# Layer 0's cross-attention: the query and key weights multiplied once, and tokens projected through the product

## The chip, the core and the metric

The kernel runs on one core of a Trainium2 chip. The metric is the device time of one execution in microseconds; 844.53 us is the median of three runs before the change (841.44 to 846.62). The core has TensorE (PE: matmuls and transposes), VectorE (DVE), ScalarE (ACT), GpSimd (POOL) and SyncE (SP), whose queue here issues all DMA transfers. Each engine works through its own list in order and waits on semaphores for the others.

## The reference

Two layers of cross-attention and feed-forward over x (8 batches of 128 tokens of 512) and a context of the same shape. The change touches only the first attention:

```
x = x + xattn0(layernorm(x), ctx)

def xattn0(text, features, Wq, bq, Wk, bk):
    Q = einsum('btx,dx->btd', text, Wq) + bq
    K = einsum('bpx,dx->bpd', features, Wk) + bk
    scores = einsum('btd,bpd->btp', Q, K) / sqrt(512)
    attn = softmax(scores, axis=-1)
    return einsum('btp,bpd->btd', attn, features)
```

Wq and Wk are 512x512; there is one head and no projection of the values. Then come a low-rank adapted FFN with a gate (layer 0), an attention with 32 query and 8 key/value heads of 128, and a gated FFN with integer weights (layer 1). Layer 1's keys and values are projected from the same context.

## The kernel before

The 1024 tokens are held as two halves of 512 (`HB` = 4 batches of `P` = 128; `KT` = 4 blocks of 128 channels). Float32 operands of the projections are split in two reduced-precision parts, h + l (`split_fast` lines 64 to 66: ScalarE casts h, VectorE subtracts to get l; `split_pool` 60 to 62 and `split_both` 68 to 70 use GpSimd), and a product is three matmuls, h·l, h·h and l·h (`mm3`, lines 77 to 80). A projection of one half is thus 4 output tiles x 4 k x 3 = 48 matmuls of 128x512.

A layer-0 half is a generator, `layer0(hf)` (line 195). Its first part normalises the tokens: statistics on VectorE (line 84, 86), the inverse deviation on GpSimd (88, 89), the normalised tokens on VectorE (95), four transposes on TensorE (101), a cast on ScalarE (107) and a remainder on VectorE (108), for each of four batches. Then it projects the half's context to keys: half 0 by `proj_first` (line 181), which goes k by k over four PSUM banks so that it can follow the loads, half 1 by `proj_T` (line 170). The bias is added where ScalarE empties PSUM (179, 193). The second part projects the tokens to queries (202). The third part multiplies queries and keys in float32 (208), takes the row maximum (212), scales it (214) and exponentiates (218). Later parts multiply by the context (236) and compute the FFN.

The loads stand ahead (lines 313 to 347): half 0's context and Wk, transposed on the host, block by block in turn; the tokens; the two biases as columns of 4; Wq. Half 1's context follows behind the first part of half 0 and is split by ScalarE and GpSimd (337). Then come FFN biases, gate and low-rank weights. The split WT (FFN) takes the place of Wk when that is done with (350).

In the built program each DMA issue on SP also waits for the landing of the transfer eight before it. Outside of the stages that are ordered by hand (from line 909) a scheduler interleaves the engines' lists. It mixes the context's projections for layer 1 (`kv_part`, line 395: matmuls `kv`, 128x256, from the split context `cT` and `wkv`) into layer 0 as filler for TensorE.

Of the kernel before, what the change touches and what calls it, by code (L numbers as in the profile page):

```python
# [21 lines left out]
HB = 4  # L22
TOK = HB * P
# [11 lines left out]
def f32(ap):  # L35
    return ap.bitcast(F32)
# [3 lines left out]
def tile_layers(ctx: ExitStack, tc: tile.TileContext, t, out: bass.AP):  # L40
    nc = tc.nc

    def pool(stack, name, bufs, space=None, side="left"):
        kw = {"side": side}
        if space is not None:
            kw["space"] = space
        return stack.enter_context(tc.tile_pool(name=name, bufs=bufs, reuse_waits="tile", **kw))

    const = pool(ctx, "const", 1)
    stage = pool(ctx, "stage", 3)  # L50
    small = pool(ctx, "small", 3)
    big = pool(ctx, "big", 2)
    dram = ctx.enter_context(tc.tile_pool(name="dram", bufs=1, space=bass.MemoryType.DRAM))
# [10 lines left out]
    def split_fast(h, lo, src):  # L64
        nc.scalar.copy(h, src)
        nc.vector.tensor_tensor(lo, src, f32(h), ALU.subtract)

    def split_both(h, lo, src):
        nc.scalar.copy(h, src)
        nc.gpsimd.tensor_tensor(lo, src, f32(h), ALU.subtract)  # L70
# [8 lines left out]
        nc.tensor.matmul(o, ah, bh, start=False, stop=False)  # L79
        nc.tensor.matmul(o, al, bh, start=False, stop=stop)  # L80

    def layernorm_stats(x):
        st = small.tile([P, 6], F32, name="bnst")
        nc.vector.bn_stats(st, x)
        mv = small.tile([P, 2], F32, name="mv")
        nc.vector.bn_aggr(mv, st)
        rstd = small.tile([P, 1], F32, name="rstd")
        nc.gpsimd.tensor_scalar(rstd, mv[:, 1:2], 1.0, LN_EPS, ALU.mult, ALU.add)
        nc.gpsimd.tensor_tensor(rstd, rstd, nhalf[:, 0:1], ALU.pow)
        return mv, rstd  # L90

    def layernorm_x(x, stats=None):
        mv, rstd = stats or layernorm_stats(x)
        xn = stage.tile([P, D], F32, name="xn", bufs=2)
        nc.vector.tensor_scalar(xn, x, mv[:, 0:1], rstd, ALU.subtract, ALU.mult)
        return xn

    def layernorm_t(xn, nh, nl, cols, ps_tr, extra=None):
        tp = ps_tr.tile([P, KT, P], F32, name="tr")
        for k in range(KT):  # L100
            nc.tensor.transpose(tp[:, k, :], xn[:, k * P : (k + 1) * P], ident)
        if nh is not None:
            layernorm_cut(tp, nh, nl, cols, extra)
        return tp
# [4 lines left out]
        if extra is not None:  # L109
            nc.scalar.copy(extra[:, :, cols], tp)  # L110

    def layernorm_T(hf, ps_tr, extra=None):

        nh = big.tile([P, KT, TOK], F32R, name="xnT_h")
        nl = big.tile([P, KT, TOK], F32R, name="xnT_l")
        for b in range(HB):
            layernorm_t(layernorm_x(xs[hf][:, b, :]), nh, nl, slice(b * P, (b + 1) * P), ps_tr, extra)
        return nh, nl


# [2 lines left out]
    xs = [const.tile([P, HB, D], F32, name=f"xs{hf}") for hf in range(2)]  # L123
# [17 lines left out]
    ps_tr = pool(sln, "ps_tr", 2, PSUM, "right")  # L141
    ps_s = pool(s0, "ps_s", 1, PSUM)
    ps_mm = pool(s0, "ps_mm", 2, PSUM)

    wts = {}

    def tile_w0(nm):
        wts[nm] = tuple(
            w0.tile([P, KT, D], F32R, name=("wq0_" if nm == "WqT" else "wkf0_") + p) for p in "hl"
        )  # L150

    tile_w0("WqT")
    tile_w0("WkT")

    def load_w0(nm, split):
# [4 lines left out]
    bq_sb = w0.tile([P, KT], F32, name="bq_sb")  # L160
    bk_sb = w0.tile([P, KT], F32, name="bk_sb")
# [18 lines left out]

    def proj_first(w, src, bias, dst):

        pss = [ps_mm.tile([P, TOK], F32, name="mm") for _ in range(2)]
        pss += [ps_kv.tile([P, 2, 2 * HD], F32, name="kv").rearrange("p a b -> p (a b)") for _ in range(2)]
        for k in range(KT):
            for j, ps in enumerate(pss):
                cols = slice(j * P, (j + 1) * P)
                mm3(
                    ps, w[0][:, k, cols], w[1][:, k, cols], src[0][:, k, :], src[1][:, k, :],
                    k == 0, k == KT - 1,  # L190
                )
        for j, ps in enumerate(pss):
            nc.scalar.activation(dst[:, j, :], ps, AF.Identity, bias=bias[:, j : j + 1])

    def layer0(hf):
        xt = xs[hf]
        xn = layernorm_T(hf, ps_tr)
        kT = l0.tile([P, KT, TOK], F32, name="k0T", bufs=2)
        (proj_T if hf else proj_first)(wts["WkT"], (cTh[hf], cTl[hf]), bk_sb, kT)
        yield  # L200
        qT = l0.tile([P, KT, TOK], F32, name="qx", bufs=2)
        proj_T(wts["WqT"], xn, bq_sb, qT)
        yield
        sp = ps_s.tile([P, HB, P], F32, name="s")
        for b in range(HB):
            cols = slice(b * P, (b + 1) * P)
# [36 lines left out]
        nh, nl = layernorm_T(hf, ps_tr, xf)  # L243
# [4 lines left out]
        for b in range(HB):  # L248
            cols = slice(b * P, (b + 1) * P)
# [53 lines left out]
        for b in range(HB):  # L303
            cols = slice(b * P, (b + 1) * P)
            ps = ps_mm.tile([P, D], F32, name="mm")
# [4 lines left out]
            nc.vector.tensor_tensor(xt[:, b, :], ps, xt[:, b, :], ALU.add)  # L310


    wk_st, cT_st = (l0.tile([P, KT, TOK], F32, name="qx", bufs=2) for _ in range(2))
    wq_st = l0.tile([P, KT, TOK], F32, name="k0T", bufs=2)
# [6 lines left out]
    nc.sync.dma_start(bk_sb, t["bk"])  # L321
    nc.sync.dma_start(bq_sb, t["bq"])
    for k in range(KT):
        nc.sync.dma_start(wq_st[:, k, :], t["WqT"][k * P : (k + 1) * P, :])
    h, lo = wts["WkT"]
    for k in range(KT):
        split_fast(cTh[0][:, k, :], cTl[0][:, k, :], cT_st[:, k, :])
        split_fast(h[:, k, :], lo[:, k, :], wk_st[:, k, :])
    h, lo = wts["WqT"]
    for k in range(KT):  # L330
        split_fast(h[:, k, :], lo[:, k, :], wq_st[:, k, :])
    A, B = layer0(0), layer0(1)
    next(A)
    c1_st = l0.tile([P, KT, TOK], F32, name="qx", bufs=2)
    for k in range(KT):
        nc.sync.dma_start(c1_st[:, k, :], t["ctxT"][k * P : (k + 1) * P, TOK : 2 * TOK])
        split_both(cTh[1][:, k, :], cTl[1][:, k, :], c1_st[:, k, :])
# [143 lines left out]
    qps, qss, rqs, qbs, pbs, q_d, p_d, qTs, sps, nms, sms, prs, tps, pTs, avs, aTs, pos = ({} for _ in range(17))  # L481
# [278 lines left out]
    for i in range(3 * NI):  # L760
        m, c = MS[i % 3], i // 3
# [38 lines left out]
    def norm_stats(b):  # L800
        xst[b] = layernorm_stats(xs[b // HB][:, b % HB, :])
# [306 lines left out]
    with tc.manual_schedule(engines={ET.PE, ET.DVE, ET.Activation, ET.Pool}):  # L1108

        c = ORDER[-1]  # L1110
# [100 lines left out]
```

## Time and profile before

| | |
|---|---|
| median of three runs | 844.53 us |
| profiled execution, its own time | 844.08 us |
| its span on the core | 842.3 us |
| TensorE busy | 820.1 us |
| VectorE busy | 634.8 us |
| DMA, mean | 196 GB/s |
| first matmul of the span | 5.19 us |
| keys of half 0, matmuls (line 193 empties them) | 5.19 to 18.5 us |
| keys of half 1, with eight transposes | 19.3 to 31.4 us |
| queries of half 0 begin | 32.91 us |
| last score of half 0 | 61.8 us |

The profile is one execution. Busy time is counted per engine, and the durations of single instructions overlap on TensorE, so the distance from one matmul to the next is the better measure there. A wait names the engine whose signal came last.

### The profile page before, as it was taken

What the parts mean: (1) busy time and instruction counts of PE and PEld (TensorE: products, weight loads), DVE (VectorE), ACT (ScalarE), POOL (GpSimd) and SP (SyncE); (2) the same over time, 40 slices, a digit from 0 to 9 for tenths busy, and PEclk for the clock granted to TensorE, in tenths of its full rate; (3) what the DMA queues carried; (4) which work ended last, traced back from release to release, by engine and by line L of the source; (5) the groups of instructions that cost most, each with busy time, mean ns of one, the idle gap of its engine ahead of it and who ended that gap; (6) DMA issues with size and microseconds to landing.
All of it is one profiled execution on the core that took longest, in us unless ns stands there. A gap on an engine that the chain in (4) does not pass through costs nothing.

```text
span 842.3 us, 14135 instructions
## 1 busy us (share of the span) xinstructions
PE 820.1 (97%) x4312; PEld 694.1 (82%) x4312; DVE 634.8 (75%) x1064; ACT 515.8 (61%) x1691; POOL 597.3 (71%) x609
## 2 busy tenths in 40 slices
PE   7999999999989999999999999999999989999996
PEld 6889998898878888888888888888888867778775
DVE  6805897675667777777777777777798897998987
ACT  6524542255666676667677666767676668755663
POOL 3713882235677887787778777888886768797686
PEclk9999999999999999999999999999999999999999
DMA  8613532274789988788888888887877602232202
GB/s 311 138 68 109 181 118 84 69 237 145 252 254 295 289 275 269 260 282 278 257 271 275 257 265 283 286 271 251 291 235 249 204 23 75 75 88 75 63 27 100
DMA packets 153564, 164.96 MB, mean 196 GB/s; under 512 B 15632, under 2 KB 94224, under 8 KB 153488
## 3 DMA queue, kind: packets, MB, share of 16 engines
q1 hardware_dynamic: 153488, 164.06, 61.3%
q8 instruction: 34, 0.56, 0.3%
q14 instruction: 42, 0.34, 0.1%
HBM read 104.78 MB, written 59.24 MB: 195 GB/s over the span
## 4 chain that ended last, share of the span: by engine, by line
PE 74%; DVE 8%; POOL 6%; DMA 5%; issue 4%; ACT 2%; SPq 1%; POOLq 0%; DVEq 0%; ACTq 0%
PE mm L78 8%; PE mm L80 8%; PE mm L79 8%; PE f L982 7%; PE f L983 7%; PE o L644 6%; PE o L647 6%; PE o L645 6%; PE s L575 5%; PE kv L78 2%; PE kv L79 2%; PE kv L80 2%; PE o L623 2%; PE o L624 1%; PE o L625 1%
## 5 line engine op out<-in xcount | busy, mean ns | idle before, releaser
L589 ACT ACTIVATE pr<-s,nm 128x128 f32<-128x128 f32 x256 | 90.5, 365 | 49.6 <-DVE nm L583 45.8
L78 PE MATMUL mm<-wq_l,xnT_h 128*128 128x512 f32 x256 | 105.6, 412 | 0.4 <-DVE q L544 0.2
L644 PE MATMUL o<-wo_l,aT_h 128*128 128x512 f32 x256 | 100.0, 391 | 2.3 <-DVE xs L652 2.3
L616 POOL TENSOR_TENSOR pT_l<-pT,pT_h 128x512 fp32r<-128x512 f32 x64 | 82.9, 1295 | 27.3 <-ACT pT_h L615 24.6
L80 PE MATMUL mm<-wq_h,xnT_l 128*128 128x512 f32 x256 | 101.3, 396 | 0.0
L79 PE MATMUL mm<-wq_h,xnT_h 128*128 128x512 f32 x256 | 100.7, 393 | 0.0
L645 PE MATMUL o<-wo_h,aT_h 128*128 128x512 f32 x256 | 99.7, 389 | 0.0
L597 POOL TENSOR_TENSOR pr<-pr,rs 128x512 f32<-128x512 f32 x64 | 67.6, 1057 | 29.4 <-DVE rs L595 29.1
L601 DVE STREAM_TRANSPOSE pb<-pr 128x512 f32<-128x512 f32 x64 | 45.5, 711 | 49.6 <-POOL pr L597 49.4
L535 ACT ACTIVATE junkq<-mm 128x128 f32<-128x128 f32 x256 | 71.6, 280 | 10.9 <-PE mm L80 4.8
L78 PE MATMUL kv<-wkv_l,cT_h 128*128 128x256 f32 x256 | 73.6, 288 | 0.0
L80 PE MATMUL kv<-wkv_h,cT_l 128*128 128x256 f32 x256 | 72.9, 285 | 0.0
L79 PE MATMUL kv<-wkv_h,cT_h 128*128 128x256 f32 x256 | 72.9, 285 | 0.0
L575 PEld LDWEIGHTS s<-kT,qT 128*128 128x128 f32 x512 | 66.9, 191 | 5.2
L673 POOL TENSOR_TENSOR qT<-qT,q 128x512 fp32r<-128x512 f32 x42 | 54.0, 1287 | 23.3 <-ACT qT L672 23.2
L647 PE MATMUL o<-wo_h,aT_l 128*128 128x512 f32 x256 | 69.0, 391 | 0.0
L366 POOL TENSOR_TENSOR rrq<-msq,nhalf 128x4 f32<-128x4 f32 x64 | 64.5, 1007 | 5.3
L575 PE MATMUL s<-kT,qT 128*128 128x128 f32 x512 | 67.4, 275 | 0.0
L615 ACT CAST pT_h<-pT 128x512 fp32r<-128x512 f32 x64 | 39.8, 622 | 41.2 <-DMA pT<-p_d 37.9
L629 ACT CAST aT_h<-o 128x512 fp32r<-128x512 f32 x64 | 37.5, 586 | 40.3 <-PE o L625 40.1
L635 DVE TENSOR_TENSOR aT_l<-o,aT_h 128x512 fp32r<-128x512 f32 x64 | 43.7, 683 | 22.8 <-ACT aT_h L629 22.7
L644 PEld LDWEIGHTS o<-wo_l,aT_h 128*128 128x128 f32 x256 | 48.1, 188 | 13.0 <-issue 2.7
(250 smaller groups left out, 2491.0 us busy)
## 6 DMA issues: line engine op xcount, KB each, us to landing
q_d<-qb SPq DMA_DIRECT2D x64, 256.0 KB, 4.1
qT<-q_d SPq DMA_DIRECT2D x64, 256.0 KB, 4.2
p_d<-pb SPq DMA_DIRECT2D x64, 256.0 KB, 2.4
pT<-p_d SPq DMA_DIRECT2D x64, 256.0 KB, 4.5
wst<-in_qpT SPq DMA_DIRECT2D x36, 256.0 KB, 4.0
wst<-in_opT SPq DMA_DIRECT2D x36, 256.0 KB, 3.1
wkv<-in_kvT SPq DMA_DIRECT2D x8, 512.0 KB, 4.1
v_d<-vh SPq DMA_DIRECT2D x16, 256.0 KB, 2.1
```

Source lines behind the costliest of these rows:

```text
L78: nc.tensor.matmul(o, ah, bl, start=start, stop=False)
L79: nc.tensor.matmul(o, ah, bh, start=False, stop=False)
L80: nc.tensor.matmul(o, al, bh, start=False, stop=stop)
L366: nc.gpsimd.tensor_tensor(r[:, :n], ms[:, :n], nhalf[:, :n], ALU.pow)
L535: nc.scalar.activation(junk, qps[u][:, r * HD : (r + 1) * HD], AF.Square, accum_out=ssq[:, r : r + 1])
L575: nc.tensor.matmul(sp[:, r, :], qTs[u][:, r, :], kTt[blocks[j]][:, :, i, :], start=True, stop=True)
L589: nc.scalar.activation(pr[:, r, :], sps[u][:, r, :], AF.Exp, bias=nms[u][:, r : r + 1], accum_out=sm[:, r : r + 1])
L597: nc.gpsimd.tensor_tensor(pr, pr, rs.unsqueeze(2).to_broadcast([P, NQ, P]), ALU.mult)
L616: nc.gpsimd.tensor_tensor(pl, tps[u], f32(ph), ALU.subtract)
L644: nc.tensor.matmul(po, ah[:, r, :], wl, start=r == 0, stop=False)
L645: nc.tensor.matmul(po, ah[:, r, :], wh, start=False, stop=False)
L647: nc.tensor.matmul(po, al[:, r, :], wo[wset[j], r][0], start=False, stop=r == NREP - 1)
```

## The change

The scores of a token x (normalised) and a context row c are (Wq x + bq)·(Wk c + bk). Written out, that is (M'x + v)·c + u·x + bq·bk, with M = Wqᵀ Wk used in its transposed sense, v = Wkᵀ bq and u = Wqᵀ bk. The new kernel

- loads Wq and Wk untransposed, splits them, and computes M once (`weight_product`: 48 matmuls in the shape of `proj_first`), and splits M out of PSUM by ScalarE and VectorE;
- projects only the tokens, through M, with v added where ScalarE empties PSUM; the raw float32 context takes the place of the keys in the score matmuls;
- gets v and u by sums of products on VectorE (`dot`, an elementwise product with a summed output) over the transposed weights, which are also loaded, and the biases, which are loaded as broadcasts to all partitions;
- sends u to DRAM and reads it back broadcast, sums it, and forms u·x for each token from the raw tokens, the kept means and inverse deviations (eight sums on VectorE, three small operations a half on GpSimd). This term is the same for a whole row of scores, as is bq·bk, which is left out. It is subtracted from the row maximum and added again.

The context's loads come after the weights, the biases and the second half's tokens; they go to the places that the transposed weights held (`k0T`), so the first waits for the sums of v, the second for those of u. WT now takes the place of Wq, and the projected tokens that of Wk.

```diff
+    def dot(junk, a, b, o):
+        nc.vector.scalar_tensor_tensor(junk, a, 1.0, b, ALU.mult, ALU.mult, accum_out=o)
+
+    def weight_product():
+        wq_, wk_ = wts["WqT"], wts["WkT"]
+        pss = [ps_mm.tile([P, D], F32, name="mm") for _ in range(2)]
+        pss += [ps_kv.tile([P, 2, 2 * HD], F32, name="kv").rearrange("p a b -> p (a b)") for _ in range(2)]
         for k in range(KT):
             for j, ps in enumerate(pss):
                 cols = slice(j * P, (j + 1) * P)
                 mm3(
+                    ps, wq_[0][:, k, cols], wq_[1][:, k, cols], wk_[0][:, k, :], wk_[1][:, k, :],
                     k == 0, k == KT - 1,
                 )
+        mh, ml = (l0.tile([P, KT, D], F32, name="qx", bufs=2).bitcast(F32R) for _ in range(2))
         for j, ps in enumerate(pss):
-            nc.scalar.activation(dst[:, j, :], ps, AF.Identity, bias=bias[:, j : j + 1])
+            split_fast(mh[:, j, :], ml[:, j, :], ps)
+        wts["M"] = mh, ml
 
     def layer0(hf):
         xt = xs[hf]
-        xn = layernorm_T(hf, ps_tr)
-        kT = l0.tile([P, KT, TOK], F32, name="k0T", bufs=2)
-        (proj_T if hf else proj_first)(wts["WkT"], (cTh[hf], cTl[hf]), bk_sb, kT)
+        xn = layernorm_T(
+            hf, ps_tr, keep=lambda b: (mvk[:, hf * HB + b, :], rsk[:, hf * HB + b : hf * HB + b + 1])
+        )
+        if hf == 0:
+            weight_product()
         yield
-        qT = l0.tile([P, KT, TOK], F32, name="qx", bufs=2)
-        proj_T(wts["WqT"], xn, bq_sb, qT)
+        kT = c_st[hf]
+        qT = w0.tile([P, KT, TOK], F32R, name="wkf0_" + "hl"[hf]).bitcast(F32)
+        proj_T(wts["M"], xn, vcol, qT)
         yield
+        bs = slice(hf * HB, (hf + 1) * HB)
+        for b in range(hf * HB, (hf + 1) * HB):
+            w = stage.tile([P, D], F32, name="wstage")
+            dot(w, xt[:, b - hf * HB, :], u_bc, trow[:, b : b + 1])
+        tm = small.tile([P, HB], F32, name="tm")
+        nc.gpsimd.tensor_scalar(tm, mvk[:, bs, 0], usum, None, ALU.mult)
+        nc.gpsimd.tensor_tensor(trow[:, bs], trow[:, bs], tm, ALU.subtract)
+        nc.gpsimd.tensor_tensor(trow[:, bs], trow[:, bs], rsk[:, bs], ALU.mult)
...
-        nc.vector.tensor_scalar(nms, nm, scale0, None, ALU.mult)
+        nc.vector.tensor_tensor(nms, nm, trow[:, bs], ALU.subtract)
+        nc.vector.tensor_tensor(nms, nms, trow[:, bs], ALU.add)
+        nc.vector.tensor_scalar(nms, nms, scale0, None, ALU.mult)
...
-        nc.sync.dma_start(cT_st[:, k, :], t["ctxT"][rows, 0:TOK])
-        nc.sync.dma_start(wk_st[:, k, :], t["WkT"][rows, :])
+        nc.sync.dma_start(wq_st[:, k, :], t["Wq"][rows, :])
+        nc.sync.dma_start(wk_st[:, k, :], t["Wk"][rows, :])
...
+    nc.sync.dma_start(bq_bc, t["bq"].to_broadcast([P, D]))
     for k in range(KT):
+        nc.sync.dma_start(wkT_st[:, k, :], t["WkT"][k * P : (k + 1) * P, :])
...
+        dot(wkT_st[:, k, :], wkT_st[:, k, :], bq_bc, vcol[:, k : k + 1])
     for b in range(HB):
         nc.sync.dma_start(xs[1][:, b, :], t["x"][HB + b])
+    nc.sync.dma_start(bk_bc, t["bk"].to_broadcast([P, D]))
+    for k in range(KT):
+        nc.sync.dma_start(wqT_st[:, k, :], t["WqT"][k * P : (k + 1) * P, :])
+        dot(wqT_st[:, k, :], wqT_st[:, k, :], bk_bc, ucol[:, k : k + 1])
+    u_d = dram.tile([1, D], F32, name="u_d")
+    nc.sync.dma_start(u_d.rearrange("o (k p) -> p (o k)", p=P), ucol)
+    u_bc = l0.tile([P, HB, P], F32R, name="p0T").bitcast(F32).rearrange("p b c -> p (b c)")
+    nc.sync.dma_start(u_bc, u_d.to_broadcast([P, D]))
+    nc.vector.tensor_reduce(usum, u_bc, AX.X, ALU.add)
+    c_st = [l0.tile([P, KT, TOK], F32, name="k0T", bufs=2) for _ in range(2)]
+    for hf in range(2):
+        for k in range(KT):
+            nc.sync.dma_start(c_st[hf][:, k, :], t["ctxT"][k * P : (k + 1) * P, hf * TOK : (hf + 1) * TOK])
+            (split_both if hf else split_fast)(cTh[hf][:, k, :], cTl[hf][:, k, :], c_st[hf][:, k, :])
```

More of the change, by code (lines that the diff above doesn't have):

```diff
@@ L80, in mm3, with layernorm_stats @@
         nc.tensor.matmul(o, al, bh, start=False, stop=stop)
-    def layernorm_stats(x):
+    def layernorm_stats(x, keep=None):
         st = small.tile([P, 6], F32, name="bnst")
         nc.vector.bn_stats(st, x)
-        mv = small.tile([P, 2], F32, name="mv")
+        mv, rstd = keep or (small.tile([P, 2], F32, name="mv"), small.tile([P, 1], F32, name="rstd"))
         nc.vector.bn_aggr(mv, st)
-        rstd = small.tile([P, 1], F32, name="rstd")
         nc.gpsimd.tensor_scalar(rstd, mv[:, 1:2], 1.0, LN_EPS, ALU.mult, ALU.add)
@@ L110, in layernorm_cut, with layernorm_T @@
             nc.scalar.copy(extra[:, :, cols], tp)
-    def layernorm_T(hf, ps_tr, extra=None):
+    def layernorm_T(hf, ps_tr, extra=None, keep=None):
         nh = big.tile([P, KT, TOK], F32R, name="xnT_h")
@@ L116, in layernorm_T @@
         for b in range(HB):
-            layernorm_t(layernorm_x(xs[hf][:, b, :]), nh, nl, slice(b * P, (b + 1) * P), ps_tr, extra)
+            st = keep and layernorm_stats(xs[hf][:, b, :], keep(b))
+            layernorm_t(layernorm_x(xs[hf][:, b, :], st), nh, nl, slice(b * P, (b + 1) * P), ps_tr, extra)
         return nh, nl
@@ L148, in tile_w0 @@
         wts[nm] = tuple(
-            w0.tile([P, KT, D], F32R, name=("wq0_" if nm == "WqT" else "wkf0_") + p) for p in "hl"
+            w0.tile([P, KT, D], F32R, name=("wkf0_" if nm == "WkT" else "wq0_") + p) for p in "hl"
         )
@@ L153, in tile_layers @@
     tile_w0("WkT")
+    mvk = w0.tile([P, NB, 2], F32, name="mvk")
+    rsk = w0.tile([P, NB], F32, name="rsk")
+    vcol = w0.tile([P, KT], F32, name="vcol")
+    ucol = w0.tile([P, KT], F32, name="ucol")
+    usum = w0.tile([P, 1], F32, name="usum")
+    trow = w0.tile([P, NB], F32, name="trow")
     def load_w0(nm, split):
@@ L158, in load_w0 @@
             load_split(t[nm][k * P : (k + 1) * P, :], h[:, k, :], lo[:, k, :], split)
-    bq_sb = w0.tile([P, KT], F32, name="bq_sb")
-    bk_sb = w0.tile([P, KT], F32, name="bk_sb")
     b0 = w0.tile([P, D], F32, name="b0")
@@ L179, in proj_T @@
             nc.scalar.activation(dst[:, j, :], ps, AF.Identity, bias=bias[:, j : j + 1])
-    def proj_first(w, src, bias, dst):
-        pss = [ps_mm.tile([P, TOK], F32, name="mm") for _ in range(2)]
+    def dot(junk, a, b, o):
[3 more added lines that the diff above has]
+        pss = [ps_mm.tile([P, D], F32, name="mm") for _ in range(2)]
         pss += [ps_kv.tile([P, 2, 2 * HD], F32, name="kv").rearrange("p a b -> p (a b)") for _ in range(2)]
@@ L188, in proj_first @@
                 mm3(
-                    ps, w[0][:, k, cols], w[1][:, k, cols], src[0][:, k, :], src[1][:, k, :],
+                    ps, wq_[0][:, k, cols], wq_[1][:, k, cols], wk_[0][:, k, :], wk_[1][:, k, :],
                     k == 0, k == KT - 1,
                 )
+        mh, ml = (l0.tile([P, KT, D], F32, name="qx", bufs=2).bitcast(F32R) for _ in range(2))
         for j, ps in enumerate(pss):
-            nc.scalar.activation(dst[:, j, :], ps, AF.Identity, bias=bias[:, j : j + 1])
+            split_fast(mh[:, j, :], ml[:, j, :], ps)
+        wts["M"] = mh, ml
     def layer0(hf):
         xt = xs[hf]
-        xn = layernorm_T(hf, ps_tr)
-        kT = l0.tile([P, KT, TOK], F32, name="k0T", bufs=2)
-        (proj_T if hf else proj_first)(wts["WkT"], (cTh[hf], cTl[hf]), bk_sb, kT)
+        xn = layernorm_T(
[3 more added lines that the diff above has]
+            weight_product()
         yield
-        qT = l0.tile([P, KT, TOK], F32, name="qx", bufs=2)
-        proj_T(wts["WqT"], xn, bq_sb, qT)
+        kT = c_st[hf]
+        qT = w0.tile([P, KT, TOK], F32R, name="wkf0_" + "hl"[hf]).bitcast(F32)
+        proj_T(wts["M"], xn, vcol, qT)
         yield
+        bs = slice(hf * HB, (hf + 1) * HB)
[6 more added lines that the diff above has]
+        nc.gpsimd.tensor_tensor(trow[:, bs], trow[:, bs], rsk[:, bs], ALU.mult)
         sp = ps_s.tile([P, HB, P], F32, name="s")
@@ L310, in layer0 @@
             nc.vector.tensor_tensor(xt[:, b, :], ps, xt[:, b, :], ALU.add)
-    wk_st, cT_st = (l0.tile([P, KT, TOK], F32, name="qx", bufs=2) for _ in range(2))
-    wq_st = l0.tile([P, KT, TOK], F32, name="k0T", bufs=2)
+    wk_st, wq_st = (l0.tile([P, KT, D], F32, name="qx", bufs=2) for _ in range(2))
     for k in range(KT):
         rows = slice(k * P, (k + 1) * P)
-        nc.sync.dma_start(cT_st[:, k, :], t["ctxT"][rows, 0:TOK])
-        nc.sync.dma_start(wk_st[:, k, :], t["WkT"][rows, :])
+        nc.sync.dma_start(wq_st[:, k, :], t["Wq"][rows, :])
+        nc.sync.dma_start(wk_st[:, k, :], t["Wk"][rows, :])
@@ L319, in tile_layers @@
     for b in range(HB):
         nc.sync.dma_start(xs[0][:, b, :], t["x"][b])
-    nc.sync.dma_start(bk_sb, t["bk"])
-    nc.sync.dma_start(bq_sb, t["bq"])
+    bq_bc, bk_bc = (l0.tile([P, D], F32R, name=f"cn_{p}", bufs=1).bitcast(F32) for p in "hl")
+    wkT_st, wqT_st = (l0.tile([P, KT, D], F32, name="k0T", bufs=2) for _ in range(2))
+    nc.sync.dma_start(bq_bc, t["bq"].to_broadcast([P, D]))
     for k in range(KT):
-        nc.sync.dma_start(wq_st[:, k, :], t["WqT"][k * P : (k + 1) * P, :])
@@ L325, in tile_layers @@
-    h, lo = wts["WkT"]
+        nc.sync.dma_start(wkT_st[:, k, :], t["WkT"][k * P : (k + 1) * P, :])
     for k in range(KT):
[L327 to L331, printed above, removed]
+        for nm, st_ in (("WqT", wq_st), ("WkT", wk_st)):
+            split_fast(wts[nm][0][:, k, :], wts[nm][1][:, k, :], st_[:, k, :])
@@ L332, in tile_layers @@
     A, B = layer0(0), layer0(1)
     next(A)
-    c1_st = l0.tile([P, KT, TOK], F32, name="qx", bufs=2)
     for k in range(KT):
-        nc.sync.dma_start(c1_st[:, k, :], t["ctxT"][k * P : (k + 1) * P, TOK : 2 * TOK])
-        split_both(cTh[1][:, k, :], cTl[1][:, k, :], c1_st[:, k, :])
+        dot(wkT_st[:, k, :], wkT_st[:, k, :], bq_bc, vcol[:, k : k + 1])
     for b in range(HB):
         nc.sync.dma_start(xs[1][:, b, :], t["x"][HB + b])
+    nc.sync.dma_start(bk_bc, t["bk"].to_broadcast([P, D]))
@@ L1175 @@
         "WkT": g["L0_xattn_Wk"].T,
-        "bq": g["L0_xattn_bq"].reshape(KT, P).T,
-        "bk": g["L0_xattn_bk"].reshape(KT, P).T,
+        "Wq": g["L0_xattn_Wq"],
+        "Wk": g["L0_xattn_Wk"],
+        "bq": g["L0_xattn_bq"].reshape(1, D),
+        "bk": g["L0_xattn_bk"].reshape(1, D),
         "WT": g["L0_ffn_W"].T,
```

## The prediction, made before the run

> **What bounds the kernel now.** I read the page first: the busy line and the slices.
>
> ```profile
> PE 820.1 (97%) x4312; PEld 694.1 (82%) x4312; DVE 634.8 (75%) x1064; ACT 515.8 (61%) x1691; POOL 597.3 (71%) x609
> PE   7999999999989999999999999999999989999996
> PEclk9999999999999999999999999999999999999999
> ```
>
> TensorE has work in nearly every slice, so a removed matmul is worth its spacing, as long as nothing else becomes late in its stage. The change touches the first 62 us. TensorE's waits (total us, times, longest), and then the busy time by stretch (columns: stretch, its length, then busy us and instructions of PE, PEld, DVE, ACT, POOL, granted clock, DMA share, GB/s):
>
> ```profile
> PE mm L78 <- DVE cT_l L66: 5.2, 1, 5.2
> PE o L644 <- DVE xs L652: 2.3, 1, 2.3
> ```
>
> ```profile
> 10.00:20.00 10.00, 10.00 (x49) 8.38 (x48) 8.40 (x18) 6.64 (x13) 6.14 (x10) 1.00 1.03 368
> 20.00:30.00 10.00, 10.00 (x49) 8.05 (x48) 9.76 (x19) 5.57 (x13) 8.60 (x13) 1.00 1.00 204
> 30.00:40.00 10.00, 10.00 (x58) 8.59 (x57) 7.95 (x12) 5.72 (x13) 8.09 (x8) 1.00 0.38 107
> 40.00:50.00 10.00, 10.00 (x54) 8.56 (x53) 1.19 (x2) 1.80 (x3) 1.90 (x2) 1.00 0.49 159
> ```
>
> TensorE waits 5.2 us for its first operands and then for no more than 0.2 at a time until 62 us. But from 10 to 40 us VectorE is busy for 26.1 of 30 us and the DMA queues are full until past 20 us: TensorE is ahead by little. The second half's 48 key matmuls (19.3 to 31.4 us in the timeline) are what it does while VectorE prepares the normalised tokens. Those are what the change removes.
>
> **What is removed.** By the built order, 96 key matmuls of 128x512 go (two halves x four output tiles x four k x three) and 48 weight-product matmuls come (four x four x three): 48 fewer. The timeline has them 0.227 us apart, so a TensorE that stays fed gains 48 x 0.227 = 10.9 us.
>
> **Where the weight product ends.** Its first matmul now needs the split of both Wq and Wk, one VectorE subtraction (0.69 us) more than before, where it started at 5.19: about 5.8. Before, 48 matmuls ended at 18.5; with that delay and the eight transposes (0.87 us) now inside, the weight product ends near 20.
>
> **When the token projection can start.** In the built order TensorE then has only transposes until the first token matmul, and that one waits for entry 48 of VectorE's list, the fourth token remainder of half 0. Before, the token projection's first matmul was at 32.91, with five context matmuls just in front of it (32.24 to 32.91) that the new order has later. VectorE's list up to there starts at 11.53, as before, and holds:
>
> - 8 statistics at 0.64 (two in 1.28) = 5.1; 8 aggregates 0.08 apart = 0.6; 6 normalisations (line 95) at 0.51 = 3.1;
> - 4 token remainders, 0.60 apart = 2.4, and the 4 new remainders of the weight product, also from PSUM, at 0.62 = 2.5;
> - 8 new sums of products over 128x512, four for each bias column. The trace has this operation with both inputs in SBUF, but with no summed output:
>
> ```profile
> L727 DVE SCALAR_TENSOR_TENSOR the<-the,qT x5: 675/680/1784, 653.9 to 690.5; 128x512 f32<-128x512 f32 x5
> ```
>
> Its median is 0.68 us. The nearest row for a summed output is ScalarE's, where reading it is 0.20 us more, so 0.68 to 0.88; I take 0.70, nearer to VectorE's own row: 8 x 0.70 = 5.6.
>
> [...]
>
> Sum: 19.3. To it come 0.45 of the wait for the inverse deviation (in the timeline at 15.09) and VectorE's losses to GpSimd, which the trace shows here:
>
> ```profile
> 19.26 1.53 DVE L95 TENSOR_SCALAR xn<-xs,mv,rstd 128x512 f32<-128x512 f32 x1 [1.15 <-POOL cT_l L70]
> ...
> 35.55 4.44 DVE L66 TENSOR_TENSOR wkv_l<-wkv,wkv_h 128x256 fp32r<-128x256 f32 x4 [0.66 <-ACT wkv_h L65]
> ```
>
> Line 95 takes 0.51 alone and 1.53 beside GpSimd's 1.38 us subtractions; four remainders of 128x256 take 1.43 alone (at 29.34) and 4.44 here. In the new order GpSimd's splits of the low-rank and FFN weights fall on the last three such entries; a loss of 0 to 1.0 each, and I take 1.0 in all. 11.5 + 19.3 + 0.45 + 1.0 = 32.3, and the projection starts near 32.4 (30.3 to 35). The remaining work of TensorE is then the same as before at 32.24: the first token matmul has moved by **+0.2 us** only, and the 10.9 us have become a hole in TensorE between 20 and 32 us. Nothing fills it: the context matmuls need the context's split, and its load is now behind Wk and Wq in both orientations, two broadcast biases and the tokens. That is 2.5 MB more at the 368 GB/s above, some 7 us later.
>
> **What the hole costs by itself.** The trace shows one idle stretch of this length, the start:
>
> ```profile
> 8.31 0.63 PE L79 MATMUL kv<-cT_h,wkf_h 128*128 128x512 f32 x1
> ...
> 10.60 0.39 PE L79 MATMUL mm<-cT_h,wkf_h 128*128 128x512 f32 x1
> 10.84 0.39 PE L78 MATMUL mm<-cT_l,wkf_h 128*128 128x512 f32 x1
> ```
>
> The first 12 matmuls are 0.43 us apart and last 0.63, all later ones 0.23 apart and 0.39, though the granted clock reads 1.00 throughout. That cost 12 x 0.20 = 2.4 us. Whether 12 us with 16 short transposes in it bring this back, no row shows: 0 to 2.6 us. I take 2.4, since the start is the only long gap of the trace.
>
> [...]
>
> **The row term.** u goes to DRAM and back as a broadcast, then VectorE sums it and makes eight more sums (5.6 us). u is written when the last column sum is done (31.5), behind the small-packet loads of the scales in SP's queue. Prices for the two trips:
>
> ```profile
> b<-in_ffn_b SPq DMA_DIRECT2D x1, 256.0 KB, 5.8
> wqn<-in_qnw SPq DMA_DIRECT2D x1, 64.0 KB, 4.4
> ...
> su_sb<-in_usT SPq DMA_DIRECT2D x1, 28.0 KB, 6.1
> sd_sb<-in_dsT SPq DMA_DIRECT2D x1, 28.0 KB, 3.9
> ```
>
> The write (512 pieces of 4 bytes) like the scales' 3.9 to 6.1, the broadcast 4.4 to 5.8: u is back at 41 to 44. VectorE reaches its first reader near 39 to 43 by the same prices, so it waits 0 to 5 us; behind it are the last two token remainders of half 1. TensorE needs these after four token groups (4 x 2.78), eight transposes (0.8), ten context matmuls and the slow start: near 46 to 48.5. So this wait is covered, with 1 to 3 us to spare. The eight sums end near 55, before the scores are complete (60). The two extra instructions on the row maximum, 0.16 us each (row of line 214), lie beside context matmuls. On ScalarE the evacuation of the first token group stands behind the first cast of half 1's context, loaded after u is sent: near 38, against TensorE's need at 39 to 41.5. For these two covers I add 0.5 us (0 to 4). What follows in layer 0 has the same instructions; the last 2913 entries of TensorE's list are the same.
>
> **Sum.** +0.2 + 2.4 + 0.5 = +3.1 us on the profiled execution's 844.1 (span 842.3), so **847 us**; the median shown, 844.53, is 0.4 above that execution. A change of under 1% (8.4 us) is within what a measurement tells from none.
>
> **Rivals.**
> - *The matmuls return at full rate* (0.30): the transposes keep TensorE awake, and the covers hold. 844.1 + 0.2, down to -2 if VectorE loses nothing to GpSimd: 842 to 845. For it: 16 transposes in the hole; against: the start.
> - *u comes back late* (0.14): VectorE stands at the reduction of u with half 1's last token remainders queued behind, and TensorE waits for these. It decides from a return later than 46 us; each us beyond costs one. With 4-byte pieces at two or three times the scales' 6.1 us it is 52 to 58: +6 to +12, plus the ramp: 852 to 858. For it: small packets, one SP queue, a write and a read in series; against: 2 KB only.
> - *TensorE stays fed* (0.04): 844.1 - 10.9 = 833. It needs VectorE to reach its entry 48 at 21 us with 19 us of work listed from 11.5 on; only if that list runs otherwise than built.
> - That the change leaves the matmuls in is excluded by the built order.
>
> My own case has 0.52. The range 842 to 854 takes in the rival without ramp and half of the late u. Faster by over 1%: 0.04; slower by over 1%: 0.13 (0.11 of the late u, above 853, and 0.02 of my own case with both covers short); the rest, 0.83, within.
>
> **What would show it.** In the new trace: a hole in TensorE from about 20 to 32 us ended by the token remainder; the first token matmul at 32.4; its first dozen spaced 0.43; the column sums at 0.70; the broadcast of u landing before 46; TensorE gapless from 33 to 62. I am wrong if context matmuls run in the hole, if the sums take over 1 us, or if a wait on u or on the context's cast stands in TensorE's list.

## The result, and the profile after

The changed kernel takes 850.8 us (median of six runs, 848.98 to 851.71); the kernel before, run beside it, 843.04 (841.44 to 846.62). The ratio is 1.0089 (95% interval 1.007 to 1.0108): 0.9% slower, with 48 matmuls fewer. The profiled execution took 851.54 us, its span 849.8 us, 7.5 us more than before's 842.3.

The same three lines of the page:

```profile
PE 816.7 (96%) x4264; PEld 687.3 (81%) x4264; DVE 648.1 (76%) x1105; ACT 514.6 (61%) x1687; POOL 602.4 (71%) x615
PE   6589999999999999999999999999999999999996
PEclk9789999999999999999999999999999999999998
```

The matmuls are gone (4312 to 4264), but the second and third of the 40 slices, 21 to 64 us, fell from full to 5 and 8 tenths. The granted clock now dips there too. TensorE's longest waits, as total us, times, longest:

```profile
PE tr L100 <- DVE xnT_l L107: 7.5, 2, 5.0
PE mm L78 <- ACT wkf_h L185: 6.5, 2, 6.0
PE mm L78 <- DVE wkf_l L66: 5.6, 1, 5.6
```

The third is the start of the kernel, 0.4 us longer than before. The first lies between the weight product and the token projection: the hole that the prediction expected. The second was not expected at this size: TensorE waits for ScalarE to empty the first token group. In TensorE's timeline (start, us, line, instruction, and in brackets the idle time before it):

```profile
21.84 1.43 PE L100 MATMUL tr<-ident,xn 128*128 128x128 f32 x8 [2.55 <-DVE xnT_l L107]
28.25 2.30 PE L100 MATMUL tr<-ident,xn 128*128 128x128 f32 x8 [4.97 <-DVE xnT_l L107]
30.20 0.78 PE L78 MATMUL mm<-xnT_l,qx 128*128 128x512 f32 x1
...
44.49 0.79 PE L78 MATMUL mm<-xnT_l,qx 128*128 128x512 f32 x1 [6.04 <-ACT wkf_h L185]
```

The projection begins at 30.20, its first six matmuls 0.43 us apart. At 44.49 it resumes after a second gap, with twelve matmuls 0.43 apart. The trace's record of the granted clock reads 0.50 from 22.73 to 32.97 us and from 43.21 to 50.03, and 1.00 elsewhere from 9.07 to 845.3. By stretches, in the columns of the prediction's table, the clock column (0.64 and 0.66) shows both:

```profile
20.00:30.00 10.00, 3.06 (x15) 2.17 (x16) 10.00 (x24) 3.25 (x6) 2.38 (x7) 0.64 1.04 275
...
40.00:50.00 10.00, 5.51 (x14) 4.35 (x15) 0.00 (x0) 2.72 (x5) 2.80 (x3) 0.66 0.60 157
```

Why ScalarE was late, from its own timeline:

```profile
43.23 0.62 ACT L69 CAST cT_h<-k0T 128x512 fp32r<-128x512 f32 x1 [8.50 <-DMA k0T<-in_ctxT]
43.76 0.68 ACT L185 ACTIVATE wkf_h<-mm,vcol 128x512 f32<-128x512 f32 x1
```

The evacuation of the first token group (line 185) stands behind the first cast of half 1's context, and that waits 8.50 us for its load. Among the DMA issues from 24 to 62 us (KB each, median us to landing):

```profile
k0T<-in_ctxT SPq DMA_DIRECT2D x4, 256.0 KB, 12.8
...
p0T<-u_d SPq DMA_DIRECT2D x1, 256.0 KB, 8.6
...
u_d<-ucol SPq DMA_DIRECT2D x1, 2.0 KB, 8.7
```

The write of u, 2 KB, takes 8.7 us to land; the context's blocks, issued just behind it, 12.8. VectorE's timeline shows u's return:

```profile
15.08 0.68 DVE L188 SCALAR_TENSOR_TENSOR k0T<-k0T,cn_h 128x512 f32<-128x512 f32 x1
15.69 0.09 DVE L188 DVE_READ_ACCUMULATOR k0T<-k0T,cn_h 128x1 f32 x1
...
51.74 0.69 DVE L369 TENSOR_REDUCE usum<-p0T 128x1 f32<-128x512 f32 x1 [13.11 <-DMA p0T<-u_d]
```

A column sum takes 0.68 us, and 0.61 passes from one to the next. The sum of u starts at 51.74, after VectorE had waited 13.1 us.

**Where the 7.5 us come from.** I took the distance from each matmul's start to the next and subtracted the median distance for a matmul of its kind (tile written and shape) in the kernel before (0.23 us for 128x512, 0.12 for 128x256, 0.11 for 128x128). What is left is TensorE's loss. "List priced" is the sum of these medians over all matmuls. Start, priced list and losses add up to the start of the last matmul. All in us, from the profiled executions; the rows below the first two are experiments of the next section:

```
kernel                      first matmul   list priced   lost to 62 us   lost after   last matmul
before                          5.19          806.9           2.3           21.1         835.4
after                           5.55          795.8          22.2           19.3         842.8
u without its trip              5.58          795.8          15.4           19.5         836.3
context cast on GpSimd          5.60          795.8          23.8           20.2         845.4
write alone, 16 pieces          5.80          795.8          14.7           18.5         834.8
hole filled                     4.83          806.9           7.0           19.3         838.0
four more sums on VectorE       5.51          795.8          18.3           17.0         836.6
v on TensorE                    5.58          799.3           6.4           21.5         832.7
fed through the hole            5.83          799.3           4.0           18.8         827.9
```

The change took 11.1 us of work away. In the 22.2 us lost before 62 us, read from the timeline, are: 1.7 of the slow start that the kernel before also has, 9.3 in the hole from 18.9 to 30.2 (the transposes' own time taken off), 1.3 in the slow matmuls behind it, 6.2 and 0.6 in two waits on ScalarE's evacuations, 2.5 in the slow dozen between them, and 0.5 in small pieces. The hole and the first slow matmuls (10.6) use up what was removed. The waits on ScalarE and the second slow dozen (9.3) make the kernel slower.

### The profile page after: what moved, and what is told of

Read it like the earlier page. It is cut to its first block, busy times and chain, and to the rows that moved or that the text cites. A ratio compares the mean times of both kernels' runs of the same rounds, so it can differ in the third digit from the quotient of the medians.

```text
span 849.8 us, 14099 instructions
## 1 busy us (share of the span) xinstructions
PE 816.7 (96%) x4264; PEld 687.3 (81%) x4264; DVE 648.1 (76%) x1105; ACT 514.6 (61%) x1687; POOL 602.4 (71%) x615
## 2 busy tenths in 40 slices
DMA packets 155388, 167.85 MB, mean 198 GB/s; under 512 B 16048, under 2 KB 94640, under 8 KB 155312
## 4 chain that ended last, share of the span: by engine, by line
PE 80%; DMA 7%; DVE 4%; issue 3%; POOL 3%; ACT 2%; SPq 1%; POOLq 0%; DVEq 0%; ACTq 0%
PE mm L78 8%; PE mm L80 8%; PE mm L79 8%; PE f L1017 7%; PE o L679 7%; PE f L1018 7%; PE o L680 6%; PE o L682 6%; PE s L610 6%; PE kv L80 3%; PE kv L79 3%; PE kv L78 3%; PE o L659 2%; PE o L658 2%; PE o L660 2%
## 5 line engine op out<-in xcount | busy, mean ns | idle before, releaser
L78 PE MATMUL mm<-wq_l,xnT_h 128*128 128x512 f32 x288 | 118.7, 412 | 0.2 <-DVE q L579 0.2
L80 PE MATMUL mm<-wq_h,xnT_l 128*128 128x512 f32 x288 | 113.8, 395 | 0.0
L79 PE MATMUL mm<-wq_h,xnT_h 128*128 128x512 f32 x288 | 113.5, 394 | 0.0
L570 ACT ACTIVATE junkq<-mm 128x128 f32<-128x128 f32 x256 | 71.8, 280 | 10.9 <-PE mm L80 4.8
L80 PEld LDWEIGHTS mm<-wq_h,xnT_l 128*128 128x128 f32 x288 | 54.1, 188 | 12.6
L78 PEld LDWEIGHTS mm<-wq_l,xnT_h 128*128 128x128 f32 x288 | 54.5, 189 | 10.0 <-ACT junkq L570 0.4
L79 PEld LDWEIGHTS mm<-wq_h,xnT_h 128*128 128x128 f32 x288 | 54.4, 189 | 9.9
```

Source lines behind the costliest of these rows:

```text
L78: nc.tensor.matmul(o, ah, bl, start=start, stop=False)
L570: nc.scalar.activation(junk, qps[u][:, r * HD : (r + 1) * HD], AF.Square, accum_out=ssq[:, r : r + 1])
```

## The experiments

Theories: (A) u's write, in 512 pieces of 4 bytes, holds up half 1's context and so TensorE; (B) the hole and its ramp (the slow matmuls behind it) are the cost, and what comes later is hidden. The line numbers in the profile lines of an experiment are those of its own kernel.

**u without its trip.**

```diff
-    u_d = dram.tile([1, D], F32, name="u_d")
-    nc.sync.dma_start(u_d.rearrange("o (k p) -> p (o k)", p=P), ucol)
...
-    nc.vector.tensor_reduce(usum, u_bc, AX.X, ALU.add)
...
-        nc.vector.tensor_tensor(nms, nm, trow[:, bs], ALU.subtract)
-        nc.vector.tensor_tensor(nms, nms, trow[:, bs], ALU.add)
```

> Left out: the row term u.x (the same for a whole row of scores), with u's way to DRAM and back, its sum, the eight sums and the small GpSimd operations. The load of the transposed Wq and the sums that give u stay, so what stands before the first token matmul is unchanged. Theory A (the write of u in 512 pieces delays half 1's context on the queue, so ScalarE's cast of it, so the evacuation of the first token group): TensorE's 6.0 us wait on the evacuation near 44 us and the second slow dozen (2.4 us) go, VectorE's 13.1 us wait goes, time near 842 (840 to 844). Theory B (the hole from 19 to 30 us and the ramp behind it are the cost, and what comes later is hidden): 848 or more.

Measured: 844.58 us, ratio 1.0015 (1.0002 to 1.0028). Most of the loss is gone, though not all that A promised (844 at most). TensorE's wait on the evacuation, of 0 to 62 us:

```profile
PE mm L78 <- ACT wkf_h L185: 1.5, 1, 1.5
```

It fell from 6.5 to 1.5 and brings no second ramp. In the table 6.8 us of the loss before 62 us go (22.2 to 15.4). B, with 848 or more, falls. What remains is near zero: the hole and its ramp cost what the matmuls gave.

**Half 1's context cast on GpSimd instead of ScalarE**, with u's trip left as it is.

```diff
-            (split_both if hf else split_fast)(cTh[hf][:, k, :], cTl[hf][:, k, :], c_st[hf][:, k, :])
+            (split_pool if hf else split_fast)(cTh[hf][:, k, :], cTl[hf][:, k, :], c_st[hf][:, k, :])
```

> Half 1's context is split by GpSimd alone, so ScalarE's evacuations of the token groups stand behind no late load; u's trip is unchanged. Theory A1 (two late paths side by side, both from the write of u: ScalarE's cast, and VectorE's wait on u with half 1's token remainders behind it): the waits on the evacuation go, TensorE now stops at half 1's first token group for a token remainder behind the sum of u, until about 54 us, and the time hardly moves: 848 to 851. Theory A2 (ScalarE's cast alone is the path): 842 to 844.

Measured: 853.3 us, ratio 1.012 (1.0103 to 1.0137). From TensorE's timeline:

```profile
54.46 0.77 PE L78 MATMUL mm<-xnT_l,qx 128*128 128x512 f32 x1 [8.51 <-DVE xnT_l L107]
```

The wait on ScalarE is gone, and one on half 1's token remainder, queued behind the sum of u on VectorE, has taken its place: 8.5 us, and a ramp behind it. So A1's two paths are there, side by side. The time is 2 us above its range: this one stop and the slow matmuls behind it lose 11.1 us, where the waits and the slow dozen of the changed kernel lose 9.3.

**Is it the write?** The run without the trip, with the write alone put back:

```diff
+    u_d = dram.tile([1, D], F32, name="u_d")
+    nc.sync.dma_start(u_d.rearrange("o (k p) -> p (o k)", p=P), ucol)
```

> The run without the trip, with only the write of u to DRAM put back (512 pieces of 4 bytes, one issue, ahead of half 1's context on the same queue); nobody reads it, and the row term stays left out. If the write itself holds up the context's loads: they land some 8 us later, ScalarE's cast of half 1 waits 7 us or more, TensorE's wait on the evacuation near 44 us is back at 4 to 6 us with a second slow dozen, time 849 to 851. If the broadcast coming back or the eight sums were what cost: time as without the trip, 844 to 845.

And the same write in the same place, as 16 pieces of 128 bytes:

```diff
-    nc.sync.dma_start(u_d.rearrange("o (k p) -> p (o k)", p=P), ucol)
+    nc.sync.dma_start(u_d.rearrange("o (r c) -> (o r) c", c=32), upad[0:16, :])
```

> The run with only the write put back, in the same place of the same queue and with the same orders on all engines, but 16 pieces of 128 bytes instead of 512 of 4 (what is written has no meaning and nobody reads it; the row term is left out). If the number of pieces is what costs: the write lands in under 4 us, the context as without the trip, time 844 to 845.5. If any write at that place costs (a wait for its landing, the turn to writing): 848 to 850.

Measured: 849.88 us, ratio 1.0084 (1.0065 to 1.0102), with 512 pieces; 843.95 us, ratio 1.0017 (1.0008 to 1.0026), with 16. The DMA issues from 24 to 62 us, first with 512 pieces:

```profile
k0T<-in_ctxT SPq DMA_DIRECT2D x4, 256.0 KB, 12.3
...
u_d<-ucol SPq DMA_DIRECT2D x1, 2.0 KB, 10.0
```

and with 16:

```profile
k0T<-in_ctxT SPq DMA_DIRECT2D x4, 256.0 KB, 3.8
...
u_d<-ucol SPq DMA_DIRECT2D x1, 2.0 KB, 2.4
```

The same 2 KB in the same place of the same queue: 10.0 us or 2.4, and the context behind it 12.3 or 3.8. All transfers together moved 16 GB/s from 37 to 44 us in the first run, and 324 from 35 to 40 us in the second. Nobody reads u in either. So the write in small pieces alone costs 0.67% (1.0084 against 1.0017), some 5.6 us, of the 0.74% by which the changed kernel stands above the run without the trip. The broadcast back, the sum and the eight sums add nothing that these runs can show as long as the write is there.

**The write on another queue**, GpSimd's, all else in the same order.

```diff
-    nc.sync.dma_start(u_d.rearrange("o (k p) -> p (o k)", p=P), ucol)
+    nc.gpsimd.dma_start(u_d.rearrange("o (k p) -> p (o k)", p=P), ucol)
```

> The changed kernel with the one write of u issued on GpSimd's queue instead of SP's; the order of all other instructions is the same. If what costs is the place in SP's queue (half 1's context issued behind the write): the context lands near 38 to 39 us, the wait on the evacuation falls to at most 1.5 us; the broadcast is issued earlier and VectorE's wait on u falls to 5 us or less, hidden: 843.5 to 846. If the small pieces hold up the DMA engines whichever queue they come from: the context still lands after 41 us and the time stays above 848.

Measured: 849.85 us, ratio 1.0082 (1.0065 to 1.0098). My main expectation was wrong. The DMA issues:

```profile
su_sb<-in_usT SPq DMA_DIRECT2D x1, 28.0 KB, 12.2
sd_sb<-in_dsT SPq DMA_DIRECT2D x1, 28.0 KB, 9.9
u_d<-ucol POOLq DMA_DIRECT2D x1, 2.0 KB, 9.9
```

The scales, on SP's queue beside the write, took 12.2 and 9.9 us instead of 5.6 and 3.3, and the four issues of the context spread over 6.71 us instead of 1.93, the first alone taking 4.45. From 33 to 38 us all transfers together moved 2 GB/s. The first cast was at 41.89. Queue order is not the reason; the write holds up transfers of another queue too. On GpSimd's queue the trace records it as 16 packets of 128 bytes, not as 512 of 4 (the whole run has 15552 packets under 512 bytes, the changed kernel 16048), though the access pattern is the same; so the size of the recorded packets does not tell this write from the harmless one of the run before, and why they differ stays open. TensorE waited 3.0 us, and some ten slow matmuls followed. VectorE's wait on u was 5.9 us.

**The context issued ahead of the write**, still with 512 pieces and the whole row term.

```diff
-    u_d = dram.tile([1, D], F32, name="u_d")
...
     for hf in range(2):
...
             (split_both if hf else split_fast)(cTh[hf][:, k, :], cTl[hf][:, k, :], c_st[hf][:, k, :])
+    u_d = dram.tile([1, D], F32, name="u_d")
+    nc.sync.dma_start(u_d.rearrange("o (k p) -> p (o k)", p=P), ucol)
...
+    nc.vector.tensor_reduce(usum, u_bc, AX.X, ALU.add)
```

> The changed kernel with nothing left out; only u's trip stands behind half 1's context in the program. In the built order the context is issued ahead of the write of u (still 512 pieces of 4 bytes), and VectorE's sum of u stands behind half 1's last token remainders. TensorE's and ScalarE's lists are unchanged. If the place of the write is what costs: the context lands near 39 us, the wait on the evacuation is at most 2 us with no second slow dozen, time 844.5 to 846.5. If the pieces still in flight slow whatever runs beside them: the context lands after 41 us and the time stays at 848 to 851.

Measured: 849.64 us, ratio 1.0074 (1.0049 to 1.0098). Neither side in full: the context came in time (first cast at 35.67), yet the time is that of the second case. ScalarE's timeline shows what was late instead:

```profile
47.60 1.32 ACT L65 CAST wkv_h<-wkv 128x256 fp32r<-128x256 f32 x4 [6.38 <-DMA wkv<-in_kvT]
```

The next block of layer 1's weights, issued at 41.46 with the write in flight until 44.8, took 6.1 us instead of 3.6; a later evacuation stands behind its cast. TensorE waited 3.7 us, and twelve slow matmuls followed. The stall moved to the next load.

**u turned on VectorE and written as 16 pieces**, row term kept; the scheduler put the context ahead of the write.

```diff
+    nc.vector.transpose(upt, upad)
+    for i in range(4):
+        nc.sync.dma_start(
+            u_d.rearrange("o (k i c) -> i (o k) c", k=KT, i=4)[i], upt[i * 32 : i * 32 + KT, :]
+        )
```

> u is turned on VectorE and written as 16 pieces of 128 bytes by four issues, where it was 512 pieces of 4 bytes by one; in the built order half 1's context is issued ahead of that write and the broadcast comes back behind the loads of wkv. Theory C (the 4-byte pieces are what is slow): half 1's context lands before ScalarE needs it, no wait on the evacuation beyond 1 us, the write lands in 2 to 4 us: time 842 to 845. Theory D (the trip through DRAM is long by itself, or late because of its place on the queue): VectorE still waits 8 us or more for u and TensorE stops at half 1's token remainder: 847 to 851.

Measured: 846.07 us, ratio 1.0038 (1.0024 to 1.0053). C holds in kind: TensorE's wait on the evacuation is 1.8 us, near the 1.5 of the run without the trip, and VectorE has no wait on u, though the broadcast is issued only at 43.19. The time is 1 us above C's range. Against the run just above, which also has the context ahead of its write and the whole row term, the long pieces gain 3.6 us. In the profiled execution a second ramp shows all the same, 1.4 us after that wait:

```profile
48.56 0.50 PE L78 MATMUL mm<-xnT_l,qx 128*128 128x512 f32 x1 [1.82 <-ACT wkf_h L188]
...
49.93 0.63 PE L80 MATMUL mm<-xnT_h,qx 128*128 128x512 f32 x1
```

Four matmuls run at the full rate (0.23 apart behind the first), then seven at 0.43 us to 52.9, which cost 1.5 us: this wait, 1.82 us, is shorter than those ahead of the other ramps behind 40 us (3.0 us and more).

**The hole filled.** 48 matmuls that nobody reads, 46 of them in the hole of the run without the trip:

```diff
+        for i in range(48):
+            nc.tensor.matmul(jp, wq_[0][:, i % KT, 0:P], wk_[0][:, i % KT, :], start=(i == 0), stop=(i == 47))
```

> The run without the trip, with 48 more matmuls of 128x512 that nobody reads, put on TensorE's list into the hole between the weight product and the token projection (46 of them spaced 0.23 are 10.6 us of a hole of 11). If the hole costs its ramp: the projection still begins near 30.2, its first matmuls are 0.23 apart instead of 0.43, and the time is 1 to 1.6 us less than without the trip: 843. If the ramp is not set by the idle time: the first matmuls stay slow and the time is the same, 844.6. If the transposes are held up by the added matmuls: up to 2 us more.

Measured: 844.98 us, ratio 1.0027 (1.0009 to 1.0045), against 1.0015 without them. TensorE's timeline:

```profile
33.20 0.48 PE L78 MATMUL mm<-xnT_l,qx 128*128 128x512 f32 x1
33.52 0.39 PE L79 MATMUL mm<-xnT_h,qx 128*128 128x512 f32 x1
```

The projection runs at the full rate from its first matmul (0.32 us to the second, then 0.23, where without the added matmuls the first eight are 0.43 apart), and the granted clock is 1.00 from 20 to 40 us, against 0.68 and 0.81 without them. In this pair of runs it is the idle time that makes the first matmuls slow. But two sets of transposes stand behind the added matmuls, and it starts at 33.20 instead of 30.24, which takes the gain back. Putting 11.1 us of matmuls back costs nothing that the intervals can tell: the removed ones were worth little or nothing in this place.

**Is VectorE's list what sets the start?** Four more sums behind those for v:

```diff
         dot(wkT_st[:, k, :], wkT_st[:, k, :], bq_bc, vcol[:, k : k + 1])
+        dot(wkT_st[:, k, :], wkT_st[:, k, :], bq_bc, trow[:, k : k + 1])
```

> The run without the trip, with four further sums of the same form on VectorE behind the four for v, into a column that nobody reads. If VectorE's list sets the start of the token projection: the first token matmul moves from 30.24 by 4 x 0.61 = 2.4 us to 32.7, and the time to 847. If something else sets it (GpSimd's inverse deviations, the transposes, a load) or the stage has slack behind it: the start moves by less than 1 us and the time stays at 844 to 845.

Measured: 844.53 us, ratio 1.0012 (0.9998 to 1.0026): no change of time, and the expected 847 was wrong. TensorE's timeline, and then VectorE's:

```profile
34.86 0.78 PE L78 MATMUL mm<-xnT_l,qx 128*128 128x512 f32 x1
```

```profile
29.98 1.48 DVE L94 TENSOR_SCALAR xn<-xs,mvk,rsk 128x512 f32<-128x512 f32 x1
...
31.98 1.40 DVE L94 TENSOR_SCALAR xn<-xs,mvk,rsk 128x512 f32<-128x512 f32 x1
```

The start did move, by 4.6 us: 2.4 from the sums, 1.8 because the two normalisations now fall beside GpSimd's splits (1.48 and 1.40 instead of 0.54 and 0.53). So VectorE's list sets it. But in the table only 2.9 us of that are still lost at 62 us (18.3 against 15.4), because five matmuls instead of eight are slow and one small wait stands behind where there were two. After 62 us TensorE then lost 2.5 us less (17.0 against 19.5). Which of the later waits gave that back I did not pursue; a loss in this stage is not wholly a loss at the end.

**v on TensorE, no column sums**, and no row term (it is the same for a whole row, so the softmax does not see it).

```diff
-    for k in range(KT):
-        dot(wkT_st[:, k, :], wkT_st[:, k, :], bq_bc, vcol[:, k : k + 1])
+        for j in range(KT):
+            for k in range(KT):
+                nc.tensor.matmul(
+                    vps[:, 0, j : j + 1], wk_st[:, k, j * P : (j + 1) * P], bq_sb[:, k : k + 1],
+                    start=(k == 0), stop=(k == KT - 1),
+                )
```

> Left out: the row term, as in the run without the trip. v comes from 16 float32 matmuls of one column on TensorE instead of sums on VectorE; the transposed weights and the broadcast biases aren't loaded (2.5 MB less), and there are no column sums. If VectorE's sums and these loads hold up the token projection: the hole after the weight product shrinks by 8 x 0.61 = 4.9 us, the context lands some 7 us earlier, no wait on its cast: 833 to 838. If the hole is set by something else (the splits of the weight product, the normalisation, GpSimd): about the time of the run without the trip, 841 to 843.

Measured: 840.94 us, ratio 0.997 (0.9954 to 0.9986), faster than before, but above my range. The projection starts at 27.20, 3.0 us earlier and not 4.9: the eight sums are gone, but the four remainders of half 0's context (2.5 us) were scheduled into their place.

**TensorE fed through the hole.** The version just above, with the load and split of layer 1's first block of key and value weights moved ahead (`kv_group` then leaves them out), so that context matmuls can run in the hole. The control gives the kernel before the same early block.

```diff
+    kv_load(0)
     c_st = [l0.tile([P, KT, TOK], F32, name="k0T", bufs=2) for _ in range(2)]
     for hf in range(2):
+        if hf:
+            kv_cut(0)
         for k in range(KT):
```

> The run with v from TensorE, with the load and the split of the first block of layer 1's key and value weights moved ahead of the context's. In the built order 49 context matmuls (5.9 us) now stand between the weight product and the token projection. If an unfed TensorE is what kept the gain of the removed matmuls away: the idle time between 20 and 28 us falls below 2.5 us, no slow matmuls at the head of the projection, and the time is 834 to 838. If VectorE stays the limit and the projection is late by as much as was filled: 840 to 842.

> Control for the fastest version: the kernel before, with the same early load and split of the first block of key and value weights. TensorE is fed there already, so if the version's gain comes from the removed matmuls, this one stays at the time of before, within 1.5 us (841 to 844.5). If loading those weights early is itself what gains: 837 to 839.

Measured: 836.38 us, ratio 0.9919 (0.9905 to 0.9933); the control 842.89, ratio 1.0001 (0.9985 to 1.0017). The gain is not that of loading a block early: the kernel before, already fed, has none. The busy time from 20 to 30 us, which was 3.06 after the change:

```profile
20.00:30.00 10.00, 10.00 (x76) 9.96 (x75) 9.11 (x17) 7.56 (x19) 6.99 (x7) 0.83 0.95 222
```

TensorE has no gap left, and the time is below that of both kernels. The list costs 7.6 us less than before's, not 11.1, because the 16 matmuls for v (32 records) take 3.5. One thing still shows, in its timeline:

```profile
20.04 2.29 PE L205 MATMUL s<-bq_sb,qx 128*128 128x1 f32 x20
...
22.66 1.40 PE L205 MATMUL s<-bq_sb,qx 128*128 128x1 f32 x12
...
24.71 0.41 PE L79 MATMUL kv<-wkv_h,cT_h 128*128 128x256 f32 x1
```

The context matmuls from 24.35 on are 0.21 us apart for some 3 us where they are 0.12 otherwise, although TensorE was never idle before them. What stands ahead of them from 20.04 on is one-column matmuls and transposes alone; the granted clock was 0.93 from 20 to 25 us and 0.73 from 25 to 30.

## Why the prediction was right or wrong

The time lay in the range (842 to 854), and the chances had most on "within 1%"; the measured +0.9% is on the upper edge of it. The likeliest value, 847.0, was 3.8 us short. That the time fell inside is in part luck: the two covers below cost 9.3 us, far outside the 0 to 4 that I gave them, and with my other terms as they stood (844.1 + 0.2 + 2.4 + 9.3) the time would have been 856, beyond the range. By its steps:

- *What is removed* (10.9 us): right; 11.1 by the priced list.
- *The weight product ends near 20, and TensorE then has only transposes*: right, 0.7 us early; its last matmul starts at 18.90 and takes 0.39.
- *The projection starts near 32.4 (30.3 to 35)*: 30.20, just outside. The 2.2 us are three terms: VectorE's part begins at 11.05 and not 11.53 (0.5), eight sums at 0.61 and not 0.70 (0.7), and the 1.0 for losses to GpSimd, whose splits began at 30.4, behind the last remainder. The place of the term was right: in the run with doubled sums, where the normalisations do fall beside the splits, they lose 0.9 each.
- *The sums* (0.70 each): the rows show 0.68, and 0.08 to 0.09 for reading the sum, which overlaps (0.61 from one to the next). The row of line 727, 0.68, carried over.
- *What the hole costs* (2.4, 0 to 2.6): the effect is right, shown by the filled hole; the size was 1.3 (six matmuls at 0.43 instead of 0.23), and between 3 and 9 slow matmuls in other runs. The row it was taken from, the kernel's start, does not show that the granted clock reads 1.00 there: the clock's record in that trace begins only at 10.26 us, where the slow matmuls end.
- *The row term*: here the prediction failed. The write was priced like the loads of the scales, 3.9 to 6.1 us, and took 8.7; the broadcast, at 4.4 to 5.8, took 8.6. The write was issued at 34.3 and not 31.5, and u was back at 51.7, not at 41 to 44 (31.5 and these prices alone add up to 39.8 to 43.4), and VectorE waited 13.1 us, not 0 to 5. The scales' row was the wrong neighbour: `sd_sb` is 512 pieces too, by its access pattern, but of 56 bytes and read, and lands in 3.3 us.
- *+0.5 us (0 to 4) for the two covers*: the term of the sum that was mis-sized. I had put ScalarE's cast "near 38, against TensorE's need at 39 to 41.5", with the context's load "after u is sent", and gave the write no effect on that load. It held it up to 43.2. The two waits on ScalarE cost 6.8 us instead of 0.5. They brought the second slow dozen (2.5), which the sum did not have at all, though the first gap had its own.
- *The sum*: my +0.2 + 2.4 was -0.1 (9.3 + 1.3 + 0.4 for a later first matmul - 11.1), the covers were 9.3 instead of 0.5, and 1.9 that I had at 0 came back (0.6 in the slow start, 1.8 after 62 us, less 0.5 in small pieces): +7.4 before rounding, against 7.5 in the spans.
- *The rival of the late u* had the right culprit and the wrong victim. u came back 5.7 us beyond its point of decision, but in the changed kernel TensorE already stood elsewhere for the same write. With the cast moved off ScalarE the rival's mechanism is what one sees, at 853.3 us, inside its 852 to 858 (of which the range held a third, not the half that I wrote).
- *Matmuls at full rate* fell with both ramps; *TensorE stays fed* (833) was not this change, but 836.4 shows what it takes.

Of what I had named as showing me wrong, one came true: a wait on the context's cast in TensorE's list (on the evacuation that stands behind that cast). And TensorE was not gapless from 33 to 62 us.

## What to carry to other kernels

Work removed from the busiest engine is worth its time only if the next work for it is ready; price the gap that it leaves and the slow matmuls behind it first, and look for filler whose operands can be there. Vectors that go through DRAM should go in few long pieces: 2 KB in 512 pieces of 4 bytes held up the megabyte behind it (12.3 us to land in the run of the write alone, 3.8 behind 16 pieces of 128 bytes), and neither another queue (849.85 us) nor another order (849.64) cured that. When a cover is thin, ask what a late transfer does to the transfers behind it, not only to its own reader.

## What was not expected of the hardware

- The write of 2.0 KB in 512 pieces took 8.7 to 10.3 us to land in the five kernels that had it, in 16 pieces 2.4. These runs change number, size and source pattern of the pieces together, so they do not say which of these counts. Many small pieces that are read are not enough: in the changed kernel `su_sb`, 1792 pieces of 16 bytes, landed in 5.6 us.
- It slowed loads on another queue as well (3.3 to 9.9 us for `sd_sb`).
- Behind 40 us, waits of 3.0 us and more on TensorE were followed by eight to twelve matmuls at 0.43 us, waits of 1.4 to 1.7 us in four runs by none, but the 1.8 us in the run with u turned and written as 16 pieces by seven. The granted clock shows these (0.66 from 40 to 50 us after the change). In the clock records of the kernels before and after, every change lies on one grid of 3.41 us: the two stretches at half clock after the change last 10.24 and 6.83 us, three and two times 3.41, and in the kernel before the clock stays at 1.00 from 10.26 to 839.7 us, 243 times 3.41. In the other runs the granted clock by stretch gives, if it knows only 1.00 and 0.50 there too, a time at half clock between 10 and 62 us that is within 0.1 us of zero to five times 3.41 (0 in the filled hole, 17.0 with the write on GpSimd's queue). The 3.0 us in the run with GpSimd's queue, with transposes and three short matmuls before it, and the 1.8 are shorter than one step of that grid. And the length of a gap alone doesn't set the number of slow matmuls: the last wait in the hole is 5.17 or 5.18 us in five of the runs, and three to nine slow matmuls follow it. That the number depends on where a gap falls in that grid as well as on its length is my reading of this; no run moved a gap alone.
- In the run fed through the hole, matmuls of a single column stood back to back for 3.7 us with transposes between them, and the context matmuls behind them were 0.21 us apart instead of 0.12, at the low clock given there.
